# The first rows of a gated cross-attention layer: loads, values and copies in another order

## Chip, core and metric

The kernel runs on one core of a Trainium2 chip. The metric is the device time of one execution in microseconds, and the time of a kernel is the median of several executions. TensorE (PE) multiplies and transposes ("turns") 128 x 128 blocks; VectorE (DVE), ScalarE (ACT) and GpSimd (POOL) work on rows; SyncE (SP) and ScalarE start transfers through hardware queues, GpSimd through a software queue. Each engine takes its own instructions strictly in order and waits on semaphores for the others.

## What is computed

The sizes are B = 8 batches, T = 512 tokens, P = 64 context rows in a batch, H = 256 columns and E = 3 experts of 512 hidden columns. All of it is float32.

```python
nx = layer_norm(x, ln_gamma, ln_beta)                     # (8, 512, 256)
q, k, v = nx @ Wq, ctx @ Wk, ctx @ Wv
weights = softmax(q @ k.T * H ** -0.5)                    # (8, 512, 64)
combined = concat([nx, weights @ v, anchor], -1)          # (8, 512, 768), anchor = cond
router_probs = softmax(combined @ router_W + router_b)    # (8, 512, 3)
h = silu(combined @ e_w1 + e_b1)                          # three experts
routed = sum_e(router_probs_e * (h_e @ e_w2_e + e_b2_e))
g = sigmoid(silu(combined @ gate_w1 + gate_b1) @ gate_w2 + gate_b2)
out = x + g * (routed @ out_w + out_b)
```

## The kernel before

The kernel works on pairs of batches, j = 0 to 3. Ahead of the pairs stands a setup, the "first rows", which is what the change touches. After it, for each pair, `gate_layer`, three times `expert_layer` and `outputs` follow; they multiply two batches as 2 x 2 blocks with seven products instead of eight, which needs differences of activations (`combine_x`, tiles T and t1 to t4) and of weights (`combine_weights`, tile ws, on GpSimd).

The order of the work is written out by hand: the body runs under a manual schedule, and each engine executes its instructions as the calls record them. A call such as `transpose_x(0)` therefore appends to PE's, VectorE's and ScalarE's queues at once. Buffers in PSUM come from two small rotations: `either` takes banks 0 to 3 in turn, and `misc` takes the spare banks 4, 6 and 7.

These are the steps of the first rows, in the order of before:

- The context (512 rows, tile `ctx_sb` in the scratch `scr_ctx`) is loaded in two halves on SP, Wk and Wq on ScalarE's queue and Wv on SP; then x of the first two batches and the weights follow on SP. The small vectors come on GpSimd's queue.
- `wake(7)` gives PE seven products of zeros (`ps_wake`) while it waits for data.
- `context_transposes` turns the context on PE half by half (`pt_ctx`) and copies each half out of PSUM into `ctxT`: the first on VectorE, the second on ScalarE. One more `wake(1)` stands between the halves.
- `transpose_weights` turns Wk and Wq, with copies on ScalarE. `join_keys` multiplies them to one matrix `wkqT`, so that scores need no separate q and k; `project(wv_sb, ...)` makes the values `vT`.
- `statistics`, `deviation` and `normalize` make the layer norm of x on VectorE, with the square root on ScalarE.
- `small_transposes` turns biases (`cols`) and cond (`condT`).
- `transpose_x` turns a batch's normalised x on PE in two blocks k of 128 columns (`pt_x`). `scale_x` applies gamma and beta while it copies out of PSUM: k = 0 on VectorE, k = 1 on ScalarE.
- `project(wkqT, ctxT, keep_m, "m")` multiplies context and joined keys (`ps_m`). `keep_m` copies column 0 of each batch to `m0` and stores the differences of the other columns to it in `mr`.
- `router_anchor`, `value_weights` (products of values and first-layer weights, `ps_vw` to `vw`) and `anchor_rows` prepare the rest. `scores(0)` multiplies `mr` and nxT (`ps_s`); softmax and `turn_weights` follow on VectorE and give `wT`.

Of the kernel before, what the change touches and what calls it, by code (L numbers as in the profile page):

```python
# [10 lines left out]
ALU = mybir.AluOpType  # L11
# [5 lines left out]
def kernel(  # L17
# [100 lines left out]
    def load_table(func):  # L118
        nc.scalar.activation(warm_t, warm_t, func)
# [32 lines left out]
    def rows_of(w):  # L152
        return w.rearrange("(k p) n -> p k n", p=P)
# [8 lines left out]
    def by_k(flat, n):  # L162
# [14 lines left out]
    rw, rw2, m0, rw_all, gamma_all = (  # L177
        scr[:, NL : NL + 3 * KH * E].rearrange("p (k e) -> p k e", e=E),
        scr[:, NL + P : NL + P + KH * TB].rearrange("p (k e) -> p k e", e=TB),
        scr[:, NL + 2 * P : NL + 2 * P + B],  # L180
        scr[:, NL + 4 * P : NL + 4 * P + H * E].rearrange("p (d e) -> p d e", e=E),
        scr[:, NL + 4 * P + H * E : NL + 4 * P + H * E + H],
    )
# [105 lines left out]
    def wake(n):  # L289

        if not ps_wake:
            ps_wake.append(misc("ps_wake"))
        for _ in range(n):
            nc.tensor.matmul(ps_wake[0][:, :P], zeros, zeros, start=True, stop=True)  # L294


    def small_transposes():
        pt = either("pt_rows")
        nc.tensor.transpose(pt[:, :NR], rows, ident[:NR, :NR])
        nc.vector.tensor_copy(cols, pt[:, :NR])  # L300
        nc.gpsimd.tensor_copy(b2T[:, :, :E], b2_c.rearrange("p e k -> p k e"))
        pt = either("pt_cond")
        for k in range(KH):
            nc.tensor.transpose(
                pt[:, k * B : (k + 1) * B], cond_sb[:, k * P : (k + 1) * P], ident[:B, :B]
            )
        nc.vector.tensor_copy(
            condT[:, :, :B], pt[:, : KH * B].rearrange("p (k b) -> p k b", b=B)
        )

    def context_transposes():
        for d in range(2):
            if d:
                wake(1)
            pt = either(f"pt_ctx_{d}").rearrange("p (k c) -> p k c", k=KH)
            for k in range(KH):
                for t in range(NX // 2):
                    nc.tensor.transpose(
                        pt[:, k, t * P : (t + 1) * P],
                        ctx_sb[:, d * (NX // 2) + t, k * P : (k + 1) * P],  # L320
                        ident,
                    )
            half = slice(d * NX // 2 * P, (d + 1) * NX // 2 * P)
            (nc.scalar.copy if d else nc.vector.tensor_copy)(ctxT[:, :, half], pt)

    def transpose_weights(dst, w_sb, name):
        pt = either(f"pt_{name}")
# [13 lines left out]
                )  # L341
            evacuate(m, ps)

    def keep_v(m, ps):
        nc.scalar.copy(vT[:, m, :], ps)

    def join_keys():

        ps = either("ps_kq").rearrange("p (m n) -> p m n", n=H)
        for m in range(KH):  # L350
            for k in range(KH):
                nc.tensor.matmul(
                    ps[:, m, :], wkT[:, k, m * P : (m + 1) * P], wqT[:, k, :],
                    start=(k == 0), stop=(k == KH - 1),
                )
        nc.scalar.copy(wkqT, ps)

    def keep_m(m, ps):
        ps = ps.rearrange("p (b c) -> p b c", c=CT)
        nc.vector.tensor_copy(m0, ps[:, :, 0])  # L360
        nc.vector.tensor_tensor(
            mr[:, m, :, 1:], ps[:, :, 1:], m0.unsqueeze(2).to_broadcast([P, B, CT - 1]), ALU.subtract
        )


# [208 lines left out]
    def transpose_x(b):  # L574
        S["nxT", b] = npool.tile([P, KH, T], F32, tag="nxT", name=f"nxT_{b}")
        for k in range(KH):
            pt = misc(f"pt_x_{b}_{k}")
            for t in range(NT):
                nc.tensor.transpose(
                    pt[:, t * P : (t + 1) * P], S["xn", b][:, t, k * P : (k + 1) * P], ident  # L580
                )
            scale_x(S["nxT", b][:, k, :], k, pt, k % 2 == 0)

    def logits(j):

# [45 lines left out]
    def combine_x(j, engine, ts=range(4)):  # L631

        b11, b21, b12, b22 = (S["nxT", 2 * j + i][:, k, :] for i in range(2) for k in range(KH))
        if 0 in ts:
            S["T", j] = work.tile([P, 3, T], F32, tag="T", name=f"T_{j}", bufs=1)
        t1, t2, t4 = (S["T", j][:, i, :] for i in range(3))
        t3 = b12
        for i, (dst, p, q) in enumerate(((t1, b12, b11), (t2, b22, t1), (t3, b22, b12), (t4, b21, t2))):
            if i in ts:
                engine.tensor_tensor(dst, p, q, ALU.subtract)  # L640

    def scores(j):


        ps = misc(f"ps_s_{j}")
        for g in range(2):
            for k in range(KH):
                for i, h in SIDES:
                    nc.tensor.matmul(  # L649
                        ps[side(i, h), g * NH : (g + 1) * NH],  # L650
                        mr[:, k, 2 * j + i, g * TB : (g + 1) * TB],
                        S["nxT", 2 * j + i][:, k, h * NH : (h + 1) * NH],
                        start=(k == 0),
                        stop=(k == KH - 1),
                    )
        w = work.tile([P, 2, NJ, TB], F32, tag="w", name=f"w_{j}", bufs=1)
        S["w", j] = w
        tokens = w.rearrange("p g j c -> p j g c")
        nc.vector.transpose(w.rearrange("p g j c -> p (g j c)"), ps)
        nc.vector.tensor_copy(logits(j)[:, 1, :], w[:, 0, :, 0])  # L660
        nc.vector.memset(w[:, 0, :, 0], 0.0)
        mx = work.tile([P, NJ], F32, tag="mx", name=f"mx_{j}")
        nc.vector.tensor_reduce(mx, tokens, AX.XY, ALU.max)
        sm = work.tile([P, NJ], F32, tag="sm", name=f"sm_{j}")
        S["sm", j] = sm
        if j == 0:
            nc.vector.tensor_tensor(w, w, by_token(mx), ALU.subtract)
            nc.scalar.activation(w, w, AF.Exp, scale=SCALE)
            return
        nmx = work.tile([P, NJ], F32, tag="nmx", name=f"nmx_{j}")  # L670
        nc.vector.tensor_scalar_mul(nmx, mx, -SCALE)
        for t in range(NJ):
            nc.scalar.activation(
                w[:, :, t, :], w[:, :, t, :], AF.Exp, bias=nmx[:, t : t + 1], scale=SCALE,
                accum_out=sm[:, t : t + 1],
            )
# [6 lines left out]
    def by_token(a):  # L683
        return a.unsqueeze(1).unsqueeze(3).to_broadcast([P, 2, NJ, TB])
# [158 lines left out]
    def nx_product(j, n, which, start=False):  # L843
        q = GROUPS[n]
        c = 2 * q
        A, Bx, T_ = S["nxT", 2 * j], S["nxT", 2 * j + 1], S["T", j]

        def a(k, d):
            return w1[:, k, (c + d) * P : (c + d + 1) * P]

        dst, lhsT, rhs = {
            1: (U, a(0, 0), A[:, 0, :]),
            2: (Y, a(1, 0), A[:, 1, :]),
            3: (Z, ws[:, S4, q, :], Bx[:, 1, :]),
            4: (U, a(1, 1), T_[:, 2, :]),
            5: (Z, ws[:, S1, q, :], T_[:, 0, :]),
            6: (U, ws[:, S2, q, :], T_[:, 1, :]),
            7: (U, a(0, 1), Bx[:, 0, :]),
        }[which]
        product(dst[n], lhsT, rhs, start=start)  # L860

# [337 lines left out]

    with tc.manual_schedule(engines=None):  # L1200
        ctx_rows = context.flatten_outer_dims().rearrange("(t p) d -> p t d", p=P)
        for d in range(2):
            half = slice(d * NX // 2, (d + 1) * NX // 2)
            nc.sync.dma_start(ctx_sb[:, half, :], ctx_rows[:, half, :])
        for w_sb, w in ((wk_sb, Wk), (wq_sb, Wq)):
            nc.scalar.dma_start(w_sb, rows_of(w))
        nc.sync.dma_start(wv_sb, rows_of(Wv))
        load_table(AF.Sqrt)
        load_x(0)
        load_x(1)  # L1210
# [4 lines left out]
            load_first(g)  # L1215

        wake(7)
        context_transposes()
        transpose_weights(wkT, wk_sb, "wk")
        transpose_weights(wqT, wq_sb, "wq")  # L1220
        statistics(0, 0, NT)
        deviation(0, 0)
        normalize(0)
        project(wv_sb, ctxT, keep_v, "v", (0,))
        join_keys()
        project(wv_sb, ctxT, keep_v, "v", (1,))
        statistics(1, 0, NT // 2)
        small_transposes()
        statistics(1, NT // 2, NT)
        transpose_x(0)  # L1230
        deviation(0, 1)
        load_router_column()
        normalize(1)
        load_table(AF.Exp)
        project(wkqT, ctxT, keep_m, "m")
        router_anchor()
        transpose_x(1)
        value_weights(0, E)
        store_router_rows(0)
        store_router_anchor()  # L1240
        combine_weights(E)
        combine_x(0, nc.vector, (0, 1))
        scores(0)
        router_column()
        spread_router_bias()
        combine_weights(0)
        spread_router_rows(0)
        value_weights(0, 0, nc.scalar.copy, False)
        anchor_rows(E)
        anchor_rows(0)  # L1250
        sum_weights(0)
        softmax(0)
        value_differences(0, 0)
        combine_x(0, nc.vector, (2,))
        turn_weights(0)
        late_scratch()
        load_anchor(1)
# [123 lines left out]
```

## Time and profile before

| | before |
|---|---|
| median of 3 runs (lowest to highest) | 462.98 us (462.89 to 463.24) |
| the profiled execution's own time | 463.12 us |
| its span, first to last instruction | 461.3 us |
| PE / VectorE / ScalarE / GpSimd busy | 456.4 / 365.2 / 214.7 / 100.4 us |
| share of PE in the chain that ended last | 95% |
| data moved by DMA | 35.27 MB |

The page tells of one profiled execution. Times inside it are counted from the span's first instruction; the execution took 1.8 us more than its span. In a timeline each line has start, duration, engine, line of the kernel, operation, what is written and read, shapes and the number of instructions merged. A float32 matmul appears as two instructions (passes) on PE, a turning of 128 columns as one. The granted clock is 0.999 over the part of the span that the record of the clock covers.

### The profile page before, as it was taken

To read this page: it belongs to the slowest core of one execution; us is meant where nothing else is said; L and a number is where in the kernel's file an instruction comes from. 1 tells how busy PE (TensorE), PEld (TensorE's weight loads), DVE (VectorE), ACT (ScalarE), POOL (GpSimd) and SP (SyncE) were. 2 spreads that over 40 slices of the span, in tenths; PEclk is the share of its full clock that TensorE was granted. 3 is DMA by queue.
4 is the path that set the end of the run, shared out by engine and by line. 5 is a ranking of instruction groups with operands and counts; after the bars stand their busy time and mean duration, and the time that the engine had idled before them with its cause. 6 is when DMAs were issued, how large, how long until landed. Compare 5 with 4: busy or idle time off the path is not lost.

```text
span 461.3 us, 4752 instructions
## 1 busy us (share of the span) xinstructions
PE 456.4 (99%) x1455; PEld 210.1 (46%) x1455; DVE 365.2 (79%) x683; ACT 214.7 (47%) x370; POOL 100.4 (22%) x149
## 2 busy tenths in 40 slices
PE   9999999999999999999999999999999999999996
PEld 7544555444444444444444444444444444444445
DVE  2988979969799669869799659879889625787973
ACT  3445683664222666556221576548221456457000
POOL 6357715001181200001072300001072300000020
PEclk9999999999999999999999999999999999999999
DMA  8975677302013326802012235702011570000013
GB/s 275 370 158 128 102 232 126 83 0 46 7 23 46 76 87 142 159 18 46 6 24 32 37 136 120 110 0 46 6 24 23 82 195 0 0 0 1 0 22 70
DMA packets 119401, 35.27 MB, mean 76 GB/s; under 512 B 106044, under 2 KB 116336, under 8 KB 118864
## 3 DMA queue, kind: packets, MB, share of 16 engines
q1 hardware_dynamic: 115312, 27.02, 28.9%
q0 software_dynamic: 2176, 7.17, 4.7%
q10 hardware_dynamic: 1888, 0.79, 0.6%
q8 instruction: 11, 0.18, 0.2%
q14 instruction: 14, 0.11, 0.1%
HBM read 27.56 MB, written 7.39 MB: 76 GB/s over the span
## 4 chain that ended last, share of the span: by engine, by line
PE 95%; DVE 4%; issue 0%
PE ps_u L796 43%; PE ps_z L796 18%; PE ps_y L796 14%; PE ps_vw L771 5%; PE ps_gu L796 3%; PE ps_w2o L501 2%; PE ps_s L649 2%; PE ps_gz L796 1%; DVE h L1072 1%; PE ps_tokens L796 1%; PE ps_wake L294 1%; DVE h L880 1%; PE ps_v L339 1%; PE ps_m L339 1%; PE ps_gy L796 1%; DVE r L1082 0%
## 5 line engine op out<-in xcount | busy, mean ns | idle before, releaser
L880 DVE TENSOR_TENSOR h<-h,pb 128x512 f32<-128x512 f32 x96 | 61.9, 694 | 6.5 <-ACT h L829 6.5
L796 PE MATMUL ps_u<-h,w2o 128*128 128x512 f32 x144 | 64.2, 595 | 0.0
L829 ACT ACTIVATE h<-h,abias 128x512 f32<-128x512 f32 x72 | 49.6, 719 | 13.5 <-DVE h L835 13.0
L796 PE MATMUL ps_u<-nxT,w 128*128 128x512 f32 x112 | 55.3, 604 | 0.0
L796 PE MATMUL ps_z<-wT,vw 64*128 64x512 f32 x104 | 49.5, 605 | 0.0
L1105 POOL TENSOR_TENSOR yb<-yb,xb 128x512 f32<-128x512 f32 x14 | 17.8, 1269 | 142.9 <-DVE yb L1104 138.8
L796 PE MATMUL ps_z<-h,w2s 128*128 128x512 f32 x96 | 42.6, 593 | 0.2 <-DVE r L1088 0.2
L796 PEld LDWEIGHTS ps_u<-h,w2o 128*128 128x128 f32 x144 | 27.0, 190 | 32.7 <-issue 29.4
L838 ACT COPY h<-ps_u 128x512 f32<-128x512 f32 x48 | 28.0, 582 | 29.4 <-PE ps_u L796 26.9
L415 POOL DMA_DIRECT2D vrd<-vw x8 | 5.0, 630 | 136.9 <-ACT vw L778 136.9
L1072 DVE TENSOR_TENSOR h<-h,h 128x1024 f32<-128x1024 f32 x24 | 34.3, 1483 | 0.0
L796 PEld LDWEIGHTS ps_u<-nxT,w 128*128 128x128 f32 x112 | 20.2, 189 | 29.5 <-issue 24.2
L829 ACT ACTIVATE h<-ps_u,abias 128x512 f32<-128x512 f32 x24 | 16.5, 688 | 29.7 <-PE ps_z L796 29.4
L796 PEld LDWEIGHTS ps_z<-h,w2s 128*128 128x128 f32 x96 | 18.1, 190 | 23.5 <-issue 21.8
L796 PE MATMUL ps_y<-nxT,w 128*128 128x512 f32 x56 | 28.6, 592 | 0.0
L796 PE MATMUL ps_z<-T,ws 128*128 128x512 f32 x56 | 28.6, 592 | 0.0
L835 DVE TENSOR_TENSOR h<-h,ps_y 128x512 f32<-128x512 f32 x24 | 16.4, 683 | 14.8 <-PE ps_y L796 14.0
L796 PE MATMUL ps_u<-wT,vw 64*128 64x512 f32 x56 | 27.8, 611 | 0.0
L796 PE MATMUL ps_y<-wT,vw 64*128 64x512 f32 x56 | 27.0, 596 | 0.0
L771 PE MATMUL ps_vw<-w,vT 128*128 128x512 f32 (+1 forms) x64 | 26.9, 542 | 0.0
L796 PE MATMUL ps_u<-T,ws 128*128 128x512 f32 x56 | 26.6, 592 | 0.0
L796 PE MATMUL ps_u<-T,w 128*128 128x512 f32 x56 | 26.6, 592 | 0.0
(229 smaller groups left out, 792.2 us busy)
## 6 DMA issues: line engine op xcount, KB each, us to landing
pb<-pd POOLq DMA_DIRECT2D x4, 1536.0 KB, 6.5
xb<-in_x_dram SPq DMA_DIRECT2D x64, 64.0 KB, 2.4
out_dram<-yb SPq DMA_DIRECT2D x56, 64.0 KB, 2.0
w<-in_L_xcond_e_w_dram SPq DMA_DIRECT2D x6, 512.0 KB, 10.1
x<-in_x_dram SPq DMA_DIRECT2D x24, 128.0 KB, 2.9
xd<-x SPq DMA_DIRECT2D x24, 128.0 KB, 2.4
xg<-xd SPq DMA_DIRECT2D x48, 64.0 KB, 2.4
scr_wa<-in_L_xcond_e_w_dram SPq DMA_DIRECT2D x3, 512.0 KB, 16.5
```

The costliest lines, as they stand in the source:

```text
L339: nc.tensor.matmul(ps, w_sb[:, k, m * P : (m + 1) * P], src[:, k, :], start=(k == 0), stop=(k == KH - 1))
L415: nc.gpsimd.dma_start(S["vrd", j][i].rearrange("e c -> c e"), S["vw", j][row_half(i), R0:])
L501: nc.tensor.matmul(ps[:, d * H : (d + 1) * H], w2T[:, k, (i + d) * P : (i + d + 1) * P], ow_sb[:, k, :], start=(k == 0), stop=(k == KH - 1),)
L649: nc.tensor.matmul(ps[side(i, h), g * NH : (g + 1) * NH], mr[:, k, 2 * j + i, g * TB : (g + 1) * TB], S["nxT", 2 * j + i][:, k, h * NH : ( ...
L771: nc.tensor.matmul(ps, vT[:, k, j * 2 * CT : (j + 1) * 2 * CT], w1[:, KH + k, n0:n1], start=(k == 0), stop=(k == KH - 1),)
L796: nc.tensor.matmul(ps, lhsT, rhs, start=start, stop=True, skip_group_check=not start)
L829: nc.scalar.activation(h, h if src is None else src, AF.Silu, bias=abias[:, c, 2 * j + i : 2 * j + i + 1])
L835: nc.vector.tensor_tensor(h, h, part, ALU.add)
L838: nc.scalar.copy(chunk(n, i, d), part)
L880: nc.vector.tensor_tensor(h, h, S["pb", j][:, i, :, 2 * q // RC, :], ALU.mult)
L1072: nc.vector.tensor_tensor(d, p, m, ALU.subtract)
L1105: nc.gpsimd.tensor_tensor(yb, yb, S["xb", 2 * j + row][:, i, :], ALU.add)
```

## The change

Five loads change places: SP now starts the first half of the context, Wk and Wq; ScalarE starts Wv and the second half of the context. The values are made by halves of the context's rows, the first half before the second half of the context is turned, and `wake(3)` stands ahead of them in place of `wake(1)`. Each half of the turned context is copied out by both engines, block k = 0 by VectorE and k = 1 by ScalarE. The joined keys are copied in two halves. The first half of the product m stands ahead of the turning of x. The copies of `cols`, `condT` and `m0`, and the scaling of the first batch's block k = 0, move from VectorE to ScalarE. The exp table is loaded later. On VectorE `mr` is written after x of the second batch is normalised. In pair 0 the third difference of x goes to the tile T ahead of the scores, and the fourth is the one that overwrites nxT in place. ScalarE copies the first value weights ahead of the exp.

```diff
@@ small_transposes, context_transposes
-        nc.vector.tensor_copy(cols, pt[:, :NR])
+        nc.scalar.copy(cols, pt[:, :NR])
...
-        nc.vector.tensor_copy(
-            condT[:, :, :B], pt[:, : KH * B].rearrange("p (k b) -> p k b", b=B)
-        )
-
-    def context_transposes():
-        for d in range(2):
-            if d:
-                wake(1)
+        nc.scalar.copy(condT[:, :, :B], pt[:, : KH * B].rearrange("p (k b) -> p k b", b=B))
+
+    def context_transposes(*ds):
+        for d in ds:
...
-            (nc.scalar.copy if d else nc.vector.tensor_copy)(ctxT[:, :, half], pt)
+            nc.vector.tensor_copy(ctxT[:, 0, half], pt[:, 0, :])
+            nc.scalar.copy(ctxT[:, 1, half], pt[:, 1, :])
@@
-    def keep_v(m, ps):
-        nc.scalar.copy(vT[:, m, :], ps)
+    def values(d):
+
+        half = slice(d * NX // 2 * P, (d + 1) * NX // 2 * P)
+        ps = either(f"ps_v_{d}").rearrange("p (m c) -> p m c", m=KH)
+        for m in range(KH):
+            for k in range(KH):
+                nc.tensor.matmul(
+                    ps[:, m, :], wv_sb[:, k, m * P : (m + 1) * P], ctxT[:, k, half],
+                    start=(k == 0), stop=(k == KH - 1),
+                )
+        nc.scalar.copy(vT[:, :, half], ps)
@@ join_keys, keep_m
-        nc.scalar.copy(wkqT, ps)
-
-    def keep_m(m, ps):
-        ps = ps.rearrange("p (b c) -> p b c", c=CT)
-        nc.vector.tensor_copy(m0, ps[:, :, 0])
+            nc.scalar.copy(wkqT[:, m, :], ps[:, m, :])
+
+    def first_column(m, ps):
+        products[m] = ps.rearrange("p (b c) -> p b c", c=CT)
+        nc.scalar.copy(m0[:, m, :], products[m][:, :, 0])
+
+    products = {}
+
+    def keep_m(m):
+        ps = products.pop(m)
         nc.vector.tensor_tensor(
...
@@ transpose_x
-            scale_x(S["nxT", b][:, k, :], k, pt, k % 2 == 0)
+            scale_x(S["nxT", b][:, k, :], k, pt, k % 2 == 0 and b > 0)
@@ combine_x (and the same swap in nx_product)
         t3 = b12
+        if j == 0:
+            t3, t4 = t4, t3
@@ scores
             nc.vector.tensor_tensor(w, w, by_token(mx), ALU.subtract)
+            value_weights(0, 0, nc.scalar.copy, False)
             nc.scalar.activation(w, w, AF.Exp, scale=SCALE)
+            value_differences(0, 0)
             return
@@ the body
-        for d in range(2):
-            half = slice(d * NX // 2, (d + 1) * NX // 2)
-            nc.sync.dma_start(ctx_sb[:, half, :], ctx_rows[:, half, :])
-        for w_sb, w in ((wk_sb, Wk), (wq_sb, Wq)):
-            nc.scalar.dma_start(w_sb, rows_of(w))
-        nc.sync.dma_start(wv_sb, rows_of(Wv))
+        halves = [slice(d * NX // 2, (d + 1) * NX // 2) for d in range(2)]
+        nc.sync.dma_start(ctx_sb[:, halves[0], :], ctx_rows[:, halves[0], :])
+        nc.scalar.dma_start(wv_sb, rows_of(Wv))
+        nc.sync.dma_start(wk_sb, rows_of(Wk))
+        nc.scalar.dma_start(ctx_sb[:, halves[1], :], ctx_rows[:, halves[1], :])
+        nc.sync.dma_start(wq_sb, rows_of(Wq))
...
         wake(7)
-        context_transposes()
+        context_transposes(0)
+        wake(3)
+        values(0)
+        context_transposes(1)
         transpose_weights(wkT, wk_sb, "wk")
         transpose_weights(wqT, wq_sb, "wq")
         statistics(0, 0, NT)
         deviation(0, 0)
         normalize(0)
-        project(wv_sb, ctxT, keep_v, "v", (0,))
+        values(1)
         join_keys()
-        project(wv_sb, ctxT, keep_v, "v", (1,))
         statistics(1, 0, NT // 2)
         small_transposes()
         statistics(1, NT // 2, NT)
+        project(wkqT, ctxT, first_column, "m", (0,))
+        deviation(0, 1)
         transpose_x(0)
-        deviation(0, 1)
         load_router_column()
         normalize(1)
-        load_table(AF.Exp)
-        project(wkqT, ctxT, keep_m, "m")
+        project(wkqT, ctxT, first_column, "m", (1,))
+        for m in range(KH):
+            keep_m(m)
         router_anchor()
         transpose_x(1)
         value_weights(0, E)
+        load_table(AF.Exp)
...
-        combine_x(0, nc.vector, (0, 1))
+        combine_x(0, nc.vector, (0, 1, 2))
         scores(0)
...
-        value_weights(0, 0, nc.scalar.copy, False)
         anchor_rows(E)
         anchor_rows(0)
         sum_weights(0)
         softmax(0)
-        value_differences(0, 0)
-        combine_x(0, nc.vector, (2,))
         turn_weights(0)
```

More of the change, by code (lines that the diff above doesn't have):

```diff
@@ L179 @@
         scr[:, NL + P : NL + P + KH * TB].rearrange("p (k e) -> p k e", e=TB),
-        scr[:, NL + 2 * P : NL + 2 * P + B],
+        scr[:, NL + 2 * P : NL + 2 * P + KH * B].rearrange("p (m b) -> p m b", b=B),
         scr[:, NL + 4 * P : NL + 4 * P + H * E].rearrange("p (d e) -> p d e", e=E),
@@ L355, in join_keys @@
                 )
-        nc.scalar.copy(wkqT, ps)
-    def keep_m(m, ps):
-        ps = ps.rearrange("p (b c) -> p b c", c=CT)
-        nc.vector.tensor_copy(m0, ps[:, :, 0])
+            nc.scalar.copy(wkqT[:, m, :], ps[:, m, :])
[5 more added lines that the diff above has]
+        ps = products.pop(m)
         nc.vector.tensor_tensor(
-            mr[:, m, :, 1:], ps[:, :, 1:], m0.unsqueeze(2).to_broadcast([P, B, CT - 1]), ALU.subtract
+            mr[:, m, :, 1:], ps[:, :, 1:], m0[:, m, :].unsqueeze(2).to_broadcast([P, B, CT - 1]), ALU.subtract
         )
@@ L846, in nx_product @@
         A, Bx, T_ = S["nxT", 2 * j], S["nxT", 2 * j + 1], S["T", j]
+        t3, t4 = Bx[:, 0, :], T_[:, 2, :]
+        if j == 0:
+            t3, t4 = t4, t3
         def a(k, d):
@@ L854, in nx_product @@
             3: (Z, ws[:, S4, q, :], Bx[:, 1, :]),
-            4: (U, a(1, 1), T_[:, 2, :]),
+            4: (U, a(1, 1), t4),
             5: (Z, ws[:, S1, q, :], T_[:, 0, :]),
             6: (U, ws[:, S2, q, :], T_[:, 1, :]),
-            7: (U, a(0, 1), Bx[:, 0, :]),
+            7: (U, a(0, 1), t3),
         }[which]
```

## Prediction

> **What bounds the kernel now.** I read the page's busy rows first, then its chain, then the waits of PE, then the timeline of PE in order of time, and last the rows of the other engines that feed it.
>
> ```profile
> PE 456.4 (99%) x1455; PEld 210.1 (46%) x1455; DVE 365.2 (79%) x683; ACT 214.7 (47%) x370; POOL 100.4 (22%) x149
> ...
> PE 95%; DVE 4%; issue 0%
> ```
>
> ```profile
> PE ps_wake L294 <- DVE warm_t L186: 1.1, 1, 1.1
> ```
>
> PE is the bound: 456.4 of 461.3 us, 95% of the chain, and the list of PE's waits up to 60 us holds one wait, the 1.1 us at the start. Busy PE is not yet proof, since ends of matmuls are modelled, so I went by starts:
>
> ```profile
> 1.06 3.35 PE L294 MATMUL ps_wake<-scr_small 128*128 128x128 f32 x14 [1.06 <-DVE warm_t L186]
> 4.35 1.09 PE L318 MATMUL pt_ctx<-ident,scr_ctx 128*128 128x128 f32 x4
> 5.23 0.64 PE L294 MATMUL ps_wake<-scr_small 128*128 128x128 f32 x2
> 5.78 1.12 PE L318 MATMUL pt_ctx<-ident,scr_ctx 128*128 128x128 f32 x4
> 6.69 0.64 PE L330 MATMUL pt_wk<-ident,scr_w 128*128 128x128 f32 x4
> 7.17 0.60 PE L330 MATMUL pt_wq<-ident,scr_w 128*128 128x128 f32 x4
> 7.61 1.95 PE L339 MATMUL ps_v<-scr_ctx,scr_w 128*128 128x512 f32 x4
> 9.39 1.89 PE L352 MATMUL ps_kq<-scr_w,scr_k 128*128 128x256 f32 x8
> 11.12 1.88 PE L339 MATMUL ps_v<-scr_ctx,scr_w 128*128 128x512 f32 x4
> 12.93 0.24 PE L299 MATMUL pt_rows<-ident,scr_small 28*128 28x28 f32 x1
> ...
> 14.14 3.60 PE L339 MATMUL ps_m<-scr_ctx,scr_k 128*128 128x512 f32 x8
> ...
> 19.86 1.93 PE L649 MATMUL ps_s<-nxT,mr 128*32 128x256 f32 x32
> ```
>
> Start to start, a 128-column pass takes 0.213 us before 6.78 us and 0.109 after; a warm 256-column pass 0.216 (L352), a 512-column one 0.429. Beyond this rate the cold part loses only 0.15 us at 4.35 and 0.12 + 0.06 at 5.78; the two halves of context landed at 4.2 and 5.7. Warm, what is lost comes in pieces of about 0.1 us where the tile's shape changes, plus 0.07 inside the first ps_v. In the whole rest one excess reaches 0.36 us (435.5), and no other passes 0.17. **So there is almost nothing to win in the first rows: the work of PE is the time.** What can be saved there is about 0.33 us cold and 0.07 warm.
>
> ```profile
> 5.47 0.69 DVE L324 COPY scr_ctx<-pt_ctx 128x512 f32<-128x512 f32 x1 [4.46 <-PE pt_ctx L318]
> 8.61 0.43 DVE L547 BATCH_NORM_STATS2 st<-x 128x6 f32<-128x256 f32 x1 [2.44 <-DMA x<-in_x_dram]
> 19.00 0.80 DVE L566 TENSOR_SCALAR nxT<-pt_x,cols 128x512 f32<-128x512 f32 x1
> ```
>
> **The change part by part**, as a walk of PE's queue with these rates.
>
> *Loads.* Five loads of 256 KB stay in five places: three on SP, two on ACT. By place they landed at 4.21, 5.74 and 6.94 (SP), 4.66 and 6.15 (ACT). Now first context half, Wk, Wq on SP; Wv, second half on ACT. x is still SP's fourth (issued 2.24, landed 8.58); later SP loads wait for landings of the same places; POOL's queue is not passed by anything. Needed: Wv at 6.5, second half at 8.4, Wk 8.8, Wq 9.2. Cost 0; cover is 1.8 us or more each. Only the first half is on the path, in its old place.
>
> *Wakes and order, cold.* PE reaches the first transposes at 4.35 and leaves at 5.23 as before. Then three wakes (six passes, 1.28) end at 6.51. Context's first copy is split: VectorE 256 columns, about 0.69 - 256 x 1.04 ns = 0.43, 5.47 to 5.90; ScalarE's half waits for VectorE's in the program and takes about 0.37 (from 0.59 for 512), to 6.3. The first values need k = 0 at 6.51 and k = 1 at 6.9: no wait. At 6.78, when the clock is full, before has done all eight context transposes and 0.05 us worth of pt_wk; after has done four and 0.27 us of a cold pass, worth 0.14 warm. Owed: 4 x 0.109 + 0.05 - 0.14 = **+0.35**. The gap at 5.78 is already in this, since after has none there.
>
> *Values by halves.* 16 passes x 0.216 against 8 x 0.429: **+0.02**. Eight more weight loads of 0.19 lie under passes of 0.216, as in L352. The 0.07 in the first ps_v came with ScalarE's context copy ending just then (6.93 + 0.59); this goes: **-0.07**. Walk: values(0) to 8.37, second context half 8.80, wk 9.24, wq 9.68, values(1) 11.40, kq 13.13. The second half's copies end at 9.40 (VectorE) and about 9.8 (ScalarE, behind vT's half, 8.55 to 9.14), needed at 9.68 and 10.1; wkT and wqT at 10.3 and 10.8, needed at 11.40.
>
> *m ahead of x.* Same matmuls; pt_rows starts at 13.2 instead of 12.93, first m 13.5, x's turning 15.2, second m 16.1, x1's turning 18.2, scores 20.1. It buys slack: VectorE's second context copy stands ahead of x0's statistics, which now start at 9.4 and not 8.61. Statistics 2.22, ScalarE's root 0.3, reciprocal and normalising 1.6: x0 ready at 13.6, needed 15.2. x1's statistics follow to 15.7, ready from 16.7 to 17.7, needed from 18.2. Cost 0; without the move x0 would be needed at 13.5.
>
> *Work moved to ScalarE.* cols, condT and twice m0 leave VectorE (0.15 to 0.17 each); x0's first scaling (0.78) too; kq's copy becomes two. ScalarE has no row for such a small copy; nearest are its roots and L388, 0.27 to 0.30. Bounds 0.15 to 0.3 each; I take 0.25. The Trainium skill (ScalarE: Activation LUTs, Rules for kernel authors) speaks against the move: "Use VectorE, not ScalarE" for simple arithmetic. The trace says equal for the large one (L570 0.78, L566 0.79) and about 0.1 more for each small one. By the rule the four small copies cost 0.4 us if exposed; by the trace's walk ScalarE's wkqT copies end at 12.9 and 13.7 against needs of 13.5 and 14.4, its m0 for the second product at 18.25, mr on VectorE at 19.0, x1's scaling at 19.75, against scores at 20.1. Hidden, with 0.3 us to spare on the last. I take 0; 0 to 0.4 stays in the range. Behind waiting small copies on ScalarE stand x1's root and the scalings; POOL's b2T waits for cols (13.9, no change).
>
> *Exp table, values of group 0, VectorE's order.* The table (1.28 + 0.2) moves from 15.46 to after the router's copy, about 20.7 to 22.1; the exp is due at 25.0. ScalarE copies the first value weights (done 24.5) before it. t3 goes ahead of scores: three subtractions, 19.8 to 21.9, and scores' turning is due at 22.0. t4 now overwrites in place, same size, same point. wT, done at 30.75 before, comes some 0.6 earlier against PE, but evidence started at 31.50 and did not wait for it. Gain 0.
>
> Sum: +0.35 + 0.02 - 0.07 = **+0.30 us**. The profiled execution took 463.12 (span 461.3 and 1.8 around it), so 463.42; that execution lies 0.14 over the median of the three runs, so 462.98 + 0.30 = **463.3**. About 0.2% (0.93 us) is what a measurement of this kernel can tell from no change, so this is none.
>
> **A rule that widens it.** The row is the clock: L318 passes at 0.213, L330 at 0.109 from 6.78. The Trainium skill (TensorE: Matmul & The Clock Gate, Part 1) says that the gate opens after a busy window of about 3.4 us which is free-running and doesn't start with the kernel. By it the cold part of one execution could end up to 3.4 us elsewhere, worth up to 1.7 us. The four times seen (462.89 to 463.24) lie within 0.35, so I take the moment as fixed, and keep an estimate of 0.4 either way for a median.
>
> **Rivals.**
> *A, slower: ScalarE's queue becomes the bound.* The root for x0 waits for statistics that start 0.8 later, and vT's half and both wkqT copies stand behind it in order; later mr hangs on an m0 copy there. For it: some 18 instructions in a row with few gaps, spare 0.65 us at first m and 0.3 at scores. Against: each step has a row. It decides when the root ends after 12.6 (walk: 11.95), or mr after 19.3. If the hops lose 1.0 us, PE stands 0.7: 462.98 + 0.30 + 0.7 = 464.0. Chance 0.14, of which 0.11 is slower by over 0.2%.
> *B, slower: the gate opens a window later,* if the copies aren't there at 6.51 and PE idles inside that window. Before idled 0.33 in it and it opened. Price half of 3.4: 465.0. Chance 0.09.
> *C, faster: it opens sooner,* as PE now has one gap instead of two. Cold time from 4.5 on is at most 2.3 us, half of it 1.15, but values then wait for copies until 5.9: about 0.7 kept, 462.6. To pass 0.2% more would have to go. Chance 0.08, of which 0.05 faster by over 0.2%.
> *The forecast* (PE order shifts, all else hidden): 0.69.
>
> So faster 0.05, within 0.2% 0.69 + 0.03 + 0.03 = 0.75, slower 0.20. Range 462.7 (forecast with the clock's 0.4 and some of C) to 464.2 (A's end); B and the outer part of C are left out.
>
> **What would show it.** Right: six wake passes at 5.23, values at 6.5, second context half at 8.4, pt_rows at 13.2, scores at 20.1, then every later PE start 0.2 to 0.3 later. VectorE's statistics at 9.4. Wrong: PE's waits naming wkqT, mr or nxT (A); passes of 128 columns at 0.21 after 6.8 (B) or at 0.11 before it (C); evidence sooner than 31.5.

## The result, and the profile after

| | before | after |
|---|---|---|
| median of 9 runs (lowest to highest) | 462.99 us (462.89 to 463.49) | 463.91 us (463.55 to 464.85) |
| ratio, 95% interval | | 1.0023 (1.0015 to 1.0031) |
| the profiled execution: time / span | 463.12 / 461.3 us | 464.85 / 462.5 us |
| median span over the runs | 461.3 us | 461.8 us |
| time around the span, mean over the runs | 1.78 us | 2.23 us |

(The last two rows of before are from the 45 runs beside a later set.) "Around the span" is the time of an execution less its span. The change costs 0.92 us (0.2%), and the interval lies clear of a ratio of 1. The forecast was +0.30. By the medians half of the loss is inside the span, and the other half lies around it, where the forecast had a constant 1.8.

The waits of PE up to 60 us had one line before and have two after:

```profile
PE ps_wake L294 <- DVE warm_t L186: 1.1, 1, 1.1
PE ps_kq L358 <- ACT scr_k L362: 0.5, 1, 0.5
```

The timeline of PE shows where the new wait stands:

```profile
4.32 1.08 PE L314 MATMUL pt_ctx<-ident,scr_ctx 128*128 128x128 f32 x4
5.20 1.48 PE L294 MATMUL ps_wake<-scr_small 128*128 128x128 f32 x6
6.48 2.24 PE L347 MATMUL ps_v<-scr_ctx,scr_w 128*128 128x256 f32 x8
8.55 0.60 PE L314 MATMUL pt_ctx<-ident,scr_ctx 128*128 128x128 f32 x4
...
9.86 1.89 PE L347 MATMUL ps_v<-scr_ctx,scr_w 128*128 128x256 f32 x8
11.59 1.03 PE L358 MATMUL ps_kq<-scr_w,scr_k 128*128 128x256 f32 x4
13.08 1.13 PE L358 MATMUL ps_kq<-scr_w,scr_k 128*128 128x256 f32 x4 [0.46 <-ACT scr_k L362]
14.14 0.24 PE L299 MATMUL pt_rows<-ident,scr_small 28*128 28x28 f32 x1
...
21.10 1.93 PE L662 MATMUL ps_s<-nxT,mr 128*32 128x256 f32 x32
```

The eight products of `ps_kq` were one group before and are two now, with an idle stretch named between them. Start to start the fifth pass stands 0.84 us behind the fourth where its neighbours stand 0.216 apart, and the sixth 0.32: 0.73 us in all. The other loss is in the first `ps_v`: the same eight passes took 2.24 us at 6.48 and 1.89 at 9.86. The clock was full only from 7.17 us (6.77 before); the first pass started at 6.48, the second at 6.91 and the third at 7.26, so one pass and a good half of the second ran at the half clock. From `pt_rows` to `ps_s` both kernels take the same, 6.93 and 6.96 us, and from `ps_s` to the end of the span 441.49 and 441.43. So within the span all is decided by the start of `pt_rows`, which is 1.21 us later.

ScalarE's timeline of the changed kernel shows the copy that PE waits for:

```profile
11.78 0.30 ACT L562 ACTIVATE sd<-mv,eps_t 128x4 f32<-128x4 f32 x1 [0.78 <-DVE mv L559]
11.99 0.56 ACT L351 COPY vT<-ps_v 128x512 f32<-128x512 f32 x1
12.66 0.37 ACT L362 COPY scr_k<-ps_kq 128x256 f32<-128x256 f32 x1
14.25 0.37 ACT L362 COPY scr_k<-ps_kq 128x256 f32<-128x256 f32 x1 [1.22 <-PE ps_kq L358]
14.52 0.19 ACT L300 COPY cols<-pt_rows 128x28 f32<-128x28 f32 x1
```

ScalarE is not late: the first join product ends at 11.59 + 1.03 = 12.62, and the copy starts at 12.66. It is the order itself that costs. The second product writes the other half of the same PSUM tile, and it starts at 13.08, when the copy of the first half has ended (12.66 + 0.37 = 13.03).

### The profile page after: what moved, and what is told of

Same layout as the page of the kernel before. It is cut to its first block, busy times and chain, and to the rows that moved or that the text cites. A ratio compares the mean times of both kernels' runs of the same rounds, so it can differ in the third digit from the quotient of the medians.

```text
span 462.5 us, 4779 instructions
## 1 busy us (share of the span) xinstructions
PE 457.2 (99%) x1467; PEld 212.1 (46%) x1467; DVE 364.7 (79%) x679; ACT 216.4 (47%) x377; POOL 100.7 (22%) x149
## 3 DMA queue, kind: packets, MB, share of 16 engines
q0 software_dynamic: 2176, 7.17, 4.6%
## 4 chain that ended last, share of the span: by engine, by line
PE 95%; DVE 4%; issue 0%; ACT 0%
PE ps_u L811 43%; PE ps_z L811 18%; PE ps_y L811 14%; PE ps_vw L786 5%; PE ps_gu L811 3%; PE ps_w2o L512 2%; PE ps_s L662 2%; PE ps_gz L811 1%; DVE h L1090 1%; PE ps_tokens L811 1%; PE ps_wake L294 1%; PE ps_v L347 1%; PE ps_m L336 1%; DVE h L898 1%; PE ps_gy L811 1%; DVE r L1100 0%
## 5 line engine op out<-in xcount | busy, mean ns | idle before, releaser
L844 ACT ACTIVATE h<-h,abias 128x512 f32<-128x512 f32 x72 | 49.6, 719 | 13.4 <-DVE h L850 12.9
```

What stands on the lines that cost most here:

```text
L844: nc.scalar.activation(h, h if src is None else src, AF.Silu, bias=abias[:, c, 2 * j + i : 2 * j + i + 1])
```

## The experiments

Each runs beside the kernel before on the same chip; medians of before were 463.05 to 463.08. "Rows" and "scores" are the starts of `pt_rows` and `ps_s` in the one profiled execution. "Clock full" is the moment in that execution from which the trace's record of the clock is full.

| kernel | median us (runs) | ratio, 95% | median span | around it, mean | clock full | rows | scores |
|---|---|---|---|---|---|---|---|
| before | 462.99 (9) | | 461.3 | 1.78 | 6.77 | 12.93 | 19.86 |
| after | 463.91 (9) | 1.0015 to 1.0031 | 461.8 | 2.23 | 7.17 | 14.14 | 21.10 |
| after, again | 464.19 (10) | 1.0013 to 1.0032 | 462.05 | 2.22 | 6.16 | 13.76 | 20.71 |
| one copy | 463.85 (13) | 1.0009 to 1.0025 | 461.5 | 2.25 | 7.14 | 13.38 | 20.81 |
| two tiles | 463.18 (13) | 0.9996 to 1.0012 | 460.8 | 2.23 | 4.04 | 12.11 | 19.06 |
| before, split copy | 464.82 (5) | 1.0032 to 1.0058 | 463.0 | 1.78 | 5.07 | 16.34 | 23.25 |
| one copy, one wake | 463.71 (21) | 1.0007 to 1.0020 | 461.5 | 2.13 | 6.90 | 13.03 | 20.46 |
| before, small moves | 462.99 (13) | 0.9992 to 1.0008 | 461.1 | 1.97 | 7.15 | 12.91 | 19.82 |
| before, Wk first | 463.06 (13) | 0.9992 to 1.0008 | 461.3 | 1.79 | 4.60 | 12.53 | 19.76 |
| two tiles, Wk first | 463.44 (20) | 1.0004 to 1.0017 | 461.3 | 2.18 | 5.18 | 12.96 | 19.92 |
| before, small moves, Wk first | 463.07 (13) | 0.9992 to 1.0009 | 461.0 | 2.07 | 5.57 | 12.58 | 19.49 |
| later part alone | 463.09 (13) | 0.9992 to 1.0008 | 461.0 | 2.04 | 5.05 | 12.57 | 19.52 |
| two tiles, one wake | 463.45 (13) | 0.9996 to 1.0012 | 461.0 | 2.25 | 5.65 | 12.60 | 19.56 |
| later part, padded | 463.22 (13) | 0.9997 to 1.0014 | 461.3 | 1.90 | 4.92 | 12.34 | 19.30 |

### The wait of the second join product

**One copy.** The changed kernel with the join copied once, as before.

```diff
-            nc.scalar.copy(wkqT[:, m, :], ps[:, m, :])
+        nc.scalar.copy(wkqT, ps)
```

> The changed kernel with one edit undone: the joined keys are copied once after both products (one copy of 512 columns) and not in two halves of 256. Theory 1 (the second product of the joined keys waits for ScalarE's copy of the first half out of the same PSUM tile; seen once as a start 0.84 us after the previous pass and 0.32 for the pass after it, where 0.216 is the rate: 0.73 us in all): the gap goes and the time falls by 0.7, to about 463.2. Rival 2 (the slowdown comes from the moment at which TensorE's clock becomes full, 7.17 us in the changed kernel's profile against 6.77 before, and from the two added wake products): the time stays within 0.2 of 463.9.

463.85, so nothing was won. The wait at `ps_kq` is gone, and another stands in PE's waits and in the timelines:

```profile
PE ps_m L336 <- ACT scr_k L362: 0.4, 1, 0.4
...
14.13 1.12 PE L336 MATMUL ps_m<-scr_ctx,scr_k 128*128 128x512 f32 x2 [0.40 <-ACT scr_k L362]
...
13.49 0.59 ACT L362 COPY scr_k<-ps_kq 128x512 f32<-128x512 f32 x1 [0.96 <-PE ps_kq L358]
```

The last line is ScalarE's: the one copy runs from 13.49 to 14.08, after 0.96 us of waiting for both products, and the first m needs it. In the kernel before, the second half of the values (1.8 us of PE) stood between the join and its first use; the change put it ahead of the join, and only the small turnings are left as cover. Splitting the copy or not chooses where the wait stands.

**Two tiles.** The changed kernel with a PSUM tile for each join product, the copies in halves as they are.

```diff
-        ps = either("ps_kq").rearrange("p (m n) -> p m n", n=H)
         for m in range(KH):
+            ps = either(f"ps_kq_{m}")[:, :H]
...
-            nc.scalar.copy(wkqT[:, m, :], ps[:, m, :])
+            nc.scalar.copy(wkqT[:, m, :], ps)
```

> The changed kernel with the two products of the joined keys in two PSUM tiles of their own, and the two half copies kept. Theory 1a (the wait belongs to the shared tile): the second product no longer waits, the time falls by 0.7 as in the kernel with one copy, to about 463.2. Theory 1b (the wait belongs to the half copies as such, ScalarE's queue being late): a wait stays somewhere at the joined keys or at the first m, and the time stays near 463.9.

463.18, which is 0.73 under the changed kernel (1.01 under its second median, below). Neither wait is there:

```profile
5.42 1.99 PE L347 MATMUL ps_v<-scr_ctx,scr_w 128*128 128x256 f32 x8
...
8.56 1.89 PE L347 MATMUL ps_v<-scr_ctx,scr_w 128*128 128x256 f32 x8
10.29 1.89 PE L358 MATMUL ps_kq<-scr_w,scr_k 128*128 128x256 f32 x8
12.11 0.24 PE L299 MATMUL pt_rows<-ident,scr_small 28*128 28x28 f32 x1
12.19 0.26 PE L304 MATMUL pt_cond<-ident,scr_small 8*128 8x8 f32 x2
12.39 1.98 PE L336 MATMUL ps_m<-scr_ctx,scr_k 128*128 128x512 f32 x4
```

The half copies are as they were, so the shared tile is the cause of the wait, which the trace puts at 0.73 us. (Each of these tiles is a whole PSUM bank, so the runs don't tell a tile from a bank.) The median span falls by more, 1.0 us; the clock's beginning, at 4.04 us in the profiled execution, is not separated from this. The median span, 460.8, is half a microsecond *under* that of before, and still the time is not.

**Before, split copy.** The kernel before with only the split (the first diff reversed).

> The kernel before with only the joined keys' copy split in two halves as in the change. Theory 1: one wait of 0.6 to 0.7 us appears before the second product, and the time is 463.0 + 0.65 = 463.6. Rival 2: no change, 463.0.

464.82: more than expected, +1.77.

```profile
8.75 1.03 PE L352 MATMUL ps_kq<-scr_w,scr_k 128*128 128x256 f32 x4
11.87 2.08 PE L352 MATMUL ps_kq<-scr_w,scr_k 128*128 128x256 f32 x4 [2.10 <-ACT scr_k L356]
13.74 2.67 PE L339 MATMUL ps_v<-scr_ctx,scr_w 128*128 128x512 f32 x4
```

Here ScalarE *is* late. It stands at the root for x (10.77), which waits for VectorE's statistics; vT's copy and then the join's first half (11.44 to 11.81) come behind. The expectation counted the copy and not what is queued ahead of it. This execution, the slowest of the five (466.51), lost a second time: behind PE's idle stretch the record of the clock goes back to half from 11.90 to 15.31, and the four `ps_v` took 2.67 us instead of 1.88.

### The cold stretch and the clock

**One copy, one wake.** As one copy, with `wake(1)` for `wake(3)`.

```diff
-        wake(3)
+        wake(1)
         values(0)
```

> The changed kernel with one copy of the joined keys and with one wake product ahead of the values instead of three. Theory of the forecast (two wakes only fill the time in which the context's half copies are made, until about 6.3): the values start when ScalarE's copy has landed, 0.2 to 0.6 us earlier at most for the first pass, and TensorE stands idle before that, so 0 to 0.2 below the kernel with one copy, 463.1. Rival (the wakes cost their own 0.85 us cold): 0.4 to 0.8 below it. Rival (the idle time delays the clock by a window): 1.5 above it.

463.71, which is 0.14 under one copy, where each kernel's runs spread over 1.4 us and more; the median spans are both 461.5. The values start at 5.83 instead of 6.46, but the copies of the context, which end at 5.77 and 6.18, hold them up, and what is gained runs at the half clock. That the two wakes cost anything is not shown.

**The changed kernel again.**

> The changed kernel once more, nothing edited, beside the others of this set. Theory 1 (the clock becomes full on a grid of windows of 3.413 us that runs freely, and not a fixed time after the first wakes): median 463.9 again, 463.5 to 464.9 in single runs; the stretch of full clock is a whole number of windows, and begins at some moment between 4 and 8 us that is not 6.77 or 7.17. The second join product waits for ScalarE's copy of the first half again, 0.6 to 0.75 us over its neighbours' distance. Theory 2 (the later clock of the changed kernel follows from its order of work): full at 7.1 to 7.2 us again.

464.19, which is 1.14 over before in this set, 0.75 of it in the median span; so the loss is 0.9 to 1.1 us, and more than half of it can lie in the span. The clock was full from 6.16 us, so neither at 6.77 nor at 7.17, and for 457.386 us. The same records give 453.973 us for before and after, 457.386 for two tiles, and 6.827 + 3.413 (half) + 450.559 for the split copy: whole multiples of 3.413 us in every one of the fourteen traces, from a beginning that lies anywhere between 4.04 and 7.17 us. The wait of the second join product was there as before, 0.73 us.

**Before, Wk first.** The kernel before, with useful work in place of its second wake.

```diff
-        context_transposes()
+        context_transposes(0)
         transpose_weights(wkT, wk_sb, "wk")
+        context_transposes(1)
```

> The kernel before with Wk's turning put between the two context halves, where the second wake stood; nothing else. Theory 1 (work of the first microseconds that replaces a wake is a gain, as far as the next load allows): Wk landed at 4.66, its four turnings run at the half clock from 5.23 to 6.1, the second context half after them to 6.9, and Wq lands by 6.2, Wv at 6.94; the values start at 7.3 to 7.4 in place of 7.61, so 462.8 (-0.2 to -0.3). Rival (Wv's landing at 6.94 and the copies out of PSUM bound the start of the values): 463.05, no change, with the first values' pass waiting for a load or a copy.

463.06, no gain. PE reached the rows 0.40 us sooner than before (with an earlier clock) and the scores only 0.10 sooner. The timelines of PE and VectorE say why:

```profile
19.76 1.07 PE L647 MATMUL ps_s<-nxT,mr 128*32 128x256 f32 x16 [0.24 <-DVE nxT L564]
```

```profile
18.30 0.68 DVE L359 TENSOR_TENSOR mr<-ps_m,scr_small 128x504 f32<-128x504 f32 x1
18.90 0.80 DVE L564 TENSOR_SCALAR nxT<-pt_x,cols 128x512 f32<-128x512 f32 x1
19.74 0.69 DVE L638 TENSOR_TENSOR T<-nxT,nxT 128x512 f32<-128x512 f32 x1
```

VectorE's chain from x's landing (8.5 us) to its second scaling ends at 19.70, and PE starts 0.06 us behind it, though it was at the rows earlier. In the kernel before the chain ends at 19.80 and PE starts at 19.86, the same 0.06 behind. So the two were level there, and a list of PE's waits doesn't show a bound that is just reached.

**Two tiles, Wk first.** The two-tile kernel with `wake(1)` and Wk's turning ahead of the first values.

> The changed kernel with the two join products in two PSUM tiles, one wake in place of three after the first context half, and Wk's turning put ahead of the first values. Theory 1 (the spread of the changed kernel comes from how many of its first eight values passes lie ahead of the full clock): with a late clock this order saves 0.3 us of wakes, with an early one it loses 0.2 to 0.3, since Wk lands only at 5.7; so single runs lie between 463.0 and 463.75, a narrower band than the 1.4 us of the two-tile kernel, and the median is near 463.0. Rival (the spread has another source, such as the landing of the loads): the band stays at 1.3 to 1.4 us, and the median at 463.2 or above. No wait at the second join product or at the first m in either.

463.44: worse than two tiles, and the band is 1.16 us, hardly narrower than 1.4. The order made new waits: 0.3 us for Wk, and, by starts, 0.4 us at the second values (the list of waits has 0.2), since only Wq's turnings are left to cover the copies of the second context half.

**Two tiles, one wake.**

> The changed kernel with the join products in two PSUM tiles and one wake in place of three after the first context half. Theory 1 (the two wakes are filler ahead of copies that end near 6.3 us): 463.05, 0.1 to 0.2 under the two-tile kernel's 463.18. Rival (without them TensorE idles in the window that decides the clock): 463.5 or more, with passes at the half clock after 7.2 us.

463.45, and not 463.05. PE's list has no new wait, but by starts it stood some 0.3 us ahead of the first values (5.91), until VectorE's copy of the context ended at 5.86. All passes from 5.65 on ran at the full clock, so the rival's sign is missing too. Between -0.14 (one copy) and +0.27 (here) the sign of this small edit isn't settled.

### The later part, and the time around the span

**Before, small moves.** The kernel before, with `cols`, `condT`, `m0` and the first batch's first scaling on ScalarE.

> The kernel before with only the small moves to ScalarE: the copies of the turned rows and conditioning, m's first column, and the two first scalings of x. Theory 1 (they stand beside TensorE's work and cost nothing): 463.05, within 0.15 of before. Theory 2 (ScalarE's queue is so full in this stretch that what it takes over delays a copy that TensorE needs): 463.4 to 463.8, and a wait of TensorE for Activation of 0.3 us or more at the first products with x.

462.99: the moves cost nothing. PE had no wait but the first.

**Before, small moves, Wk first.** Both edits.

> The kernel before with both the small moves to ScalarE and Wk's turning in place of the second wake, which alone gave 462.99 and 463.06. Theory 1 (in the kernel before, VectorE's chain from x's landing to its second scaling is a second bound at the first scores, as long as TensorE's; so time won by TensorE ahead of it is given back there): with both, TensorE reaches the turned rows at 12.4 to 12.7 and the scores 6.9 us after them with no wait for nxT, so 462.65 (0.3 to 0.5 under before). Rival (something else holds the scores or the end): 463.0, no more than either alone.

463.07, so theory 1's gain of 0.3 to 0.5 is not in the time, but its steps are all there: rows at 12.58, scores 6.91 us behind them without a wait. The median span is 461.0, 0.3 under before. The 0.3 us came back outside the span, where this kernel has 2.07 us and before 1.79.

**Later part alone.** Everything of the change from `small_transposes` on; the loads, turnings, values and join as before.

> The kernel before with the later part of the change alone: half of m ahead of x's turning, the small copies and both first scalings on ScalarE, VectorE's order and the table's place; the loads, the turnings of context, the values and the join products with one copy stand as before. Theory 1 (the later part costs nothing, the whole loss is in the first 13 us): 463.0, within 0.15 of before, and no wait of TensorE but the first. Rival (the later part carries a share of the loss): 463.3 or more.

463.09: no share of the loss within the span (461.0), and 2.04 us around it. VectorE's second scaling here ends at 18.32 + 0.81 = 19.13, 0.6 us ahead of its end in the kernel with Wk first, at nearly the same rows:

```profile
18.32 0.81 DVE L569 TENSOR_SCALAR nxT<-pt_x,cols 128x512 f32<-128x512 f32 x1
```

What happens around the span is in the DMA records. This is the view of DMA from 455 to 466 us in before, in the later part alone and in the changed kernel, in 40 slices of 0.275 us (the span ends at 461.3, 461.0 and 462.5):

```profile
GB/s 0 97 142 131 89 157 177 101 169 129 162 77 222 17 0 203 65 0 0 0 0 0 0 0 0 0 0 0 0 0 0 0 0 0 0 0 0 0 0 0
q14 instruction: 1, 0.01, 0.2%
```

```profile
GB/s 74 143 130 98 140 183 110 167 144 115 127 196 43 0 169 69 0 0 0 0 0 0 0 0 0 0 0 0 30 0 0 0 0 0 0 0 0 0 0 0
q14 instruction: 1, 0.01, 0.3%
```

```profile
GB/s 0 0 0 0 0 0 124 137 129 85 178 164 105 179 91 197 52 224 4 9 222 8 0 0 0 0 0 0 0 0 0 0 0 30 30 0 0 0 0 0
q14 instruction: 2, 0.02, 0.6%
```

The single 30 in the second view and the two in the third are loads of instructions of 8 KB each, which start 1.7 us and more behind the last instruction of the span. Before has its last one at 459.44, ahead of the span's end. In all ten traces that have such a late load, the execution's time is the end of the last load less 0.23 to 0.25 us, while the time around the span varies from 1.97 to 2.32; in before, Wk first and split copy the load ends 1.2 to 1.6 us ahead of the span's end, and the time around the span is 1.77 to 1.78. The last output lands 1.33 us ahead of the span's end in all fourteen traces, so it is not the output. This points to the late load of code as what sets when the execution counts as done. The loads that look like VectorE's lie on average some 127 recorded instructions of VectorE apart, and the last stands at VectorE's 831st of 834 in before; the kernels with a late one record 827 or 828 for VectorE.

**Later part, padded.** Ten more instructions on VectorE while it idles; they compute nothing that is used.

```diff
         wake(7)
+        pad = const.tile([P, 1], F32, tag="pad", name="pad")
+        for _ in range(10):
+            nc.vector.memset(pad, 0.0)
```

> The kernel with the later part of the change alone, which gave 463.09 with 461.0 of span (medians), and ten one-element memsets more on VectorE while it idles at 1.5 to 4 us. Theory 1 (part of the changed kernel's loss lies outside the span: fewer VectorE instructions put the last load of instructions, 8 KB on queue q14, from 1.2 us or more ahead of the span's end to 2.2 us and more behind it, and the time of a run then reaches to that load's end): with ten instructions more it lies ahead of the end again, the time around the span falls from 2.04 to 1.78, steady within 0.05 from run to run as in the kernel before, and the median is 462.8, with the span unchanged at 461.0. Rival (the time around the span has another source, such as ScalarE's instructions, of which this kernel has more than before): around the span 2.0 to 2.1 as without the memsets, and 463.1.

The last load moved from 462.78 to 456.36, at VectorE's 830th instruction of 837, and the loads at 152.0, 216.1 and 364.0 came 2.5 to 7.3 us earlier, while those at 165.6 and 299.4 stayed. So the last load is VectorE's. The time around the span fell from 2.04 to 1.90 and became steady (standard deviation 0.04 instead of 0.08), so about half of the excess over 1.78 is the load's; theory 1 expected all of it to go. The other 0.12 us has a source that these runs don't show. The median didn't fall, 463.22, since the median span was 461.3 this time and not 461.0. In the profiled execution PE had a gap of 0.28 us ahead of 72.1 us, which the kernel without the memsets hasn't; whether that is what the median shows stays open.

## Why the prediction's walk held, and why it was short by 0.6 us

- **The number** lies in the stated range, 462.7 to 464.2, but by luck: the forecast with the clock's 0.4 reaches 463.7, and only rival A's end takes in 463.91. Two terms that the sum had at nothing, 0.73 and 0.45 us, outweigh the 0.30 that it had.
- **The walk of PE's queue** held where it was a walk: wakes at 5.20 (5.23 forecast), values at 6.48 (6.5), second context half at 8.55 (8.4), VectorE's statistics at 9.53 (9.4), scores 6.96 us after the rows (6.9). With the clock full at nearly the same moment (7.14 and 7.15), the changed front without its join wait reaches the rows at 13.38 and the old one at 12.91, +0.47, of which 0.1 to 0.2 is the context's earlier landing in the latter (3.97 against 4.16). So +0.30 was near, at 0.3 to 0.4.
- **The step that failed first: "kq's copy becomes two", taken as hidden** because "ScalarE's wkqT copies end at 12.9 and 13.7 against needs of 13.5 and 14.4". The first need was not m at 13.5. It was the second join product, due at 12.3 by the same walk, which writes into the tile that the first copy reads. That term was 0 and is 0.73. Rival A had the wait's place (wkqT on ScalarE) and almost its price (0.7), with the wrong reason: it made ScalarE late, and ScalarE was on time.
- **"1.8 around it" as a constant** failed: it is 1.78 before and 2.23 after. Part of the 0.45, some 0.15 by the padded kernel, is a load of VectorE's instructions that slipped behind the end, as the change took six of them away. The later part of the change alone has 0.26 of the 0.45. The rest comes with the changed front; several of its traces have a second late load, which isn't traced to an engine.
- **"I take the moment as fixed"** failed too. The row said 6.77 in one execution and 7.17 in the next. The Trainium skill (TensorE: Matmul & The Clock Gate, Part 1) says that the window is free-running, and that the transition varies, by half a microsecond either way, with where in it the first matmul falls. The fourteen traces agree with the window, at 3.413 us, but their beginnings spread over 3.1 us, from 4.04 to 7.17, with the first matmul at 1.06 in all. The narrow band of before (462.89 to 463.24) was read as a steady clock. The runs point to a floor instead: an early clock gains nothing there, because VectorE holds the scores at 19.7, as in the kernel with Wk first. The lowest span of before in 45 runs is 461.1, and the three kernels that free VectorE without touching the front's order of values go down to 460.6 and 460.7. The changed kernel has no such floor, and its two traces fit a time that follows the clock: full from 7.17 and from 6.16, rows at 14.14 and 13.76.
- **The sum.** In the profiled pair the span grew by 1.19: 0.73 for the join, and 0.46 for the walk and a later clock together, which that pair doesn't separate (with the forecast's 0.30 for the walk, 0.16 is left for the clock). Over the medians it grew by 0.5 in the first set and 0.75 in the second, less than in the pair; executions with an early clock, which gain in the changed kernel and not in the old one, would explain this. With 0.45 around the span this makes the 0.92 and the 1.14, to within 0.06.
- **The small copies**, taken as 0.25 each against VectorE's 0.15 to 0.17, took 0.19 (`cols`, `condT`) and 0.17 (`m0`). Moving them costs nothing, as forecast.

No version beats the kernel before by what can be measured. The two-tile kernel has the shortest median span of all, 460.8 against 461.3, and gives it back around the span, 2.23 against 1.78.

## What to carry to other kernels

When a product and its copy are split in halves to start the next step sooner, look at what else uses the tile: in this kernel halves in one PSUM tile chained matmul, copy and matmul (0.73 us), while halves in two tiles overlapped. A narrow band of times is no proof of a steady cause; it can be a second engine that is level with the first, and then gains on the first are lost until the second is freed as well. When a span shrinks and the time doesn't, compare the time around the span, and look for the last load of instructions.

## What was not expected of the hardware

- The last load of instructions, 8 KB on q14, can lie up to 2.55 us behind the last instruction, and the execution's time then reached to its end less 0.23 to 0.25 us in ten traces. With ten more instructions on VectorE this load came 6.4 us sooner.
- The stretch of full clock was a whole number of windows of 3.413 us in every trace. In the one trace with an idle stretch of 2.1 us on PE (9.78 to 11.87), the half clock came back at 11.90 for exactly one window.
